# Selective-scan layers on one core: the side work of every third unit is issued ahead of the next unit's B and decay

## The chip, the cores and the metric

The kernel runs on one core of one Trainium2 chip. The metric is the device time of one execution in microseconds. It is compared with the time of the kernel before the change, run on the same chip.

The core has five engines with a queue each: TensorE (PE in the profile, PEld for its weight loads), VectorE (DVE), ScalarE (ACT), GpSimd (POOL) and SyncE (SP), which only issues DMA transfers here. An instruction waits in its engine's queue until the semaphores that it needs have been raised.

## The reference

Four layers, each adding a two-dimensional selective scan to its input `x` (8 images, 48 by 48 positions, 96 channels). Cut to what matters:

```
for each layer:
    g = group_norm(x)
    xc, z = split(g @ in_proj)                     # 192 channels each
    xc = silu(depthwise_conv3x3(xc) + conv_b)
    xs = 4 sequences of xc: by rows, by columns, and both backwards      # L = 2304
    dt, B, C = split(xs @ x_proj)                  # rank 6 or 16; 16 states; 16 states
    delta = softplus(dt @ dt_proj + bias)
    for each position, channel and state n:
        h = exp(delta * A[n]) * h + (delta * u) * B[n]
        y += h * C[n]
    y = layer_norm(sum of the 4 directions + D * u) * silu(z)
    x = x + y @ out_proj
```

The last layer writes the same recurrence with cumulative sums and an epsilon. The kernel computes it only at the two ends of each sequence, and a test at the end decides whether a full pass has to follow.

## The kernel before, in words

Images are worked in pairs. A pair's 2 x 192 channels fill three tiles of 128 partitions. For each tile there are two scan orders (rows, columns) and two directions, 12 groups in all. A group's 2,304 positions are cut into three chunks of 768. Inside a chunk a **unit** n = 0 to 15 handles one pair of states of one half of the tile: 128 partitions by 768 positions. Layers 0 to 2 ("long" layers) have 3 layers x 4 pairs x 12 groups x 3 chunks x 16 = 6,912 units. The last layer ("short") has small units of another form, which the change leaves alone.

Work of a unit in a long layer:

- `load_b` and `load` (through `fetch`, L740) have SP issue the DMAs of B and C, broadcast over the partitions. C comes for every unit, into one of nine buffers `cb`. B comes by DMA only in **pooled** units, n = 2, 5, 7, 10, 13, 15 (`pooled`), into one of three buffers `bb`.
- In pooled units POOL multiplies B by delta*u (`weigh`, L757), and ACT writes the decay exp(delta*A) into PSUM (`spread` calling `exp`, L780).
- In the other units ACT writes the decay into one of four buffers `da` (`decay`, L780). TensorE spreads B over the partitions from its bf16 parts (`spread`, L678: four matmuls into one of two PSUM buffers `b`, the same two buffers that the pooled units' decay uses). DVE multiplies B by delta*u (L810).
- `scan`: DVE runs the recurrence (L814), POOL multiplies the result by C (L823, `c*h`), and a last column is put on a list that `catch_up` has ACT copy later (L698).
- `add_up`: TensorE sums the products of a pair of units into PSUM (L870; L855 begins a sum). It runs `LAG` = 2 units behind. `collect` has ACT copy a finished sum into `y` (L887).

Beside the units run two kinds of other work, given out in small steps:

- **The softplus step** (`prepare`, a generator, `coming` in the loop) makes delta and delta*u for the next chunk but one or the next. It works on two halves of 384 columns, by steps s1 to s7 and s8 to s15: s1 and s8 the matmuls of dt (L614); s2 and s9 three ACT operations (L622 to L624); s3 and s10 three more (L626 to L628, the last two giving `w1`); s4 and s11 the matmuls of `e` and `w1` (L634, eight instructions); s5 and s12 those of `lg` and `x` (L634, eight); s6 and s13 four ACT copies of delta (L589), in s6 also the DVE product with u (L642 or L645); s14 the second half's DVE product; s7 and s15 four ACT copies of delta*u. The generator is started again at n = 15 of a chunk, where s1 is issued, and one step follows in each unit, so that s2 comes at n = 0 and s15 at n = 13.
- **The side step** (`side_step`) takes one step of the next pair's prologue (`ahead`, or `rest` at the start: input projection, the convolution's matmuls at L314, the projections and their stores) or of the last pair's epilogue (`behind`: normalization and output projection, with matmuls at L1031 to L1119, ACT operations, two DVE products at L1086 and L1108, and its loads and stores on SP). No side step is taken in the unit where `ends` holds, which is n = 2.

The order is written out by hand in `run`. One turn of its loop issues, for unit k: `collected()` (a late sum's copy), `get_ready(k + 1)` (loads for units k+5 and k+4, spread of unit k+1, weigh and decay of unit k+3), `catch_up()`, `scan` of unit k, `add_up` of unit k-2, and then, by `beside()`, the softplus step and the side step. Where a late sum has been copied (n = 3), `beside()` stands ahead of `add_up`. `keep_order` adds a dependency from each instruction of an engine to the one before it for all of the long layers, so that each engine runs them in the order in which the program issues them.

Of the kernel before, what the change touches and what calls it, by code (L numbers as in the profile page):

```python
# [103 lines left out]
def ss2d_layers_kernel(ctx: ExitStack, tc: tile.TileContext, x_in, consts, weights, out):  # L104
# [470 lines left out]
    def load_dt(c):  # L575
        r = layers[c.l].rank
        c.dts = sm1.tile([64, SCAN], F32, name="dts", tag="dts")
        for b in c.batches:
            q0 = 32 * b if c.t == 2 else 0
            nc.sync.dma_start(  # L580
                c.dts[q0 : q0 + r, : c.m],
                state[c.l, c.p]["xd"][c.ph, b, c.d * r : (c.d + 1) * r, c.c0 : c.c0 + c.m],
            )
# [101 lines left out]
    def store_some(n):  # L685
        for _ in range(min(n, len(late_stores))):
            o, z, at = late_stores.pop(0)
            nc.sync.dma_start(o[:, at], z[:, at])

    def collected():  # L690
        some = bool(late_sums)
        while late_sums:
            late_sums.pop(0)()
        return some

    def catch_up():
        while late_act:
            nc.scalar.copy(*late_act.pop(0))  # L698
# [450 lines left out]
    def drain(g):  # L1149
        for _ in g:  # L1150
            pass

    def step(g):
        next(g, None)
# [7 lines left out]
    def side_step(*sides):  # L1162

        for s in sorted(sides, key=lambda s: (not s.held, s.made / s.total)):
            got = next(s.g, s)
            s.held = got is True
            if got is not s and got is not GATED:
                s.made += 1
                return True
        return False  # L1170
# [3 lines left out]
    def mark():  # L1174
        marks.append(len(tc._region_blocks()[0].instructions))
# [12 lines left out]
    LAG = 2  # L1188
    LOADS, DECAYS = 3, 2

    def run(pairs, short):


        def units():
            for l, p in pairs:
                for gi, (t, ph, d) in enumerate(groups):
                    if l in short:
                        c = Edge(l, p, t, ph, d)
                        for i in range(NS // QUAD):
                            yield (l, p, gi * (NS // QUAD) + i), c, i  # L1200
                        continue
                    group = {}
                    for i in range(len(SCANS)):
                        c = Chunk(l, p, t, ph, d, i, group, c if d == 1 and i == 0 else None)
                        for n in range(NS):
                            yield (l, p, (gi * len(SCANS) + i) * NS + n), c, n

        def begin(l, p, first=False):
            if l not in layers:
                layers[l] = Layer(l)  # L1210
            return prologue(l, p, l in short, first)

        todo = list(units())

        def rest_of_sum(k):
            before = todo[k - 1][1] if k > 0 else None
            if isinstance(before, Chunk) and (k == len(todo) or todo[k][1] is not before):
                before.add_up(NS)

        def get_ready(k):  # L1220

            def early(ahead, what):
                for i in range(0 if k == 0 else k + ahead, min(k + ahead + 1, len(todo))):
                    getattr(todo[i][1], what)(todo[i][2])

            early(LOADS + 1, "load_b")
            early(LOADS, "load")
            if k == 0:
                todo[0][1].decay(todo[0][2])
            if k < len(todo):  # L1230
                (l, p, _), c, n = todo[k]
                if n == 0 and c.first and l not in short:
                    c.group["carry"] = capool.tile([P, NS], F32, name="carry", tag="carry")
                c.spread(n)
            early(DECAYS, "weigh")
            for i in range(k + DECAYS if k else 1, min(k + DECAYS + 1, len(todo))):
                todo[i][1].decay(todo[i][2])

        rest = begin(*pairs[0], first=True)
        while next(rest) is not READY:  # L1240
            pass
        rest = Side(rest)
        chunks = list(dict.fromkeys(c for _, c, _ in todo))
        drain(prepare(chunks[0]))
        behind = ahead = Side()
        coming = iter(())
        done = None
        mark()
        get_ready(0)
        for k, ((l, p, unit), c, n) in enumerate(todo):  # L1250
            at = pairs.index((l, p))
            following = pairs[at + 1] if at + 1 < len(pairs) else None
            if l in short and unit == 0:
                mark()
            per = NS // QUAD if l in short else NS
            all_units = len(groups) * (per if l in short else len(SCANS) * per)
            place["tiles"] = 3 * unit // all_units
            store_some(1)
            if done:
                behind, done = Side(epilogue(*done), 199), None  # L1260
            if unit == LAG and following:
                ahead = Side(begin(*following), 311)
            if k == 0:
                coming_to = 1
                coming = prepare(chunks[coming_to])
            if n == max(0, per - 1 - DECAYS):
                while coming_to < len(chunks) and not chunks[coming_to].ready:
                    next(coming)
            if n == 10 and coming_to + 1 < len(chunks):
                z = chunks[coming_to + 1]  # L1270
                if (z.l, z.p) == (l, p):
                    load_dt(z)
            busy = collected()
            get_ready(k + 1)
            catch_up()
            c.scan(n)
            if n == per - 1:
                drain(coming)
                if unit + 1 + per == all_units:
                    drain(behind.g)  # L1280
                    drain(ahead.g)
                coming_to = chunks.index(c) + 2
                coming = prepare(chunks[coming_to]) if coming_to < len(chunks) else iter(())


            def beside():
                step(coming)

                for _ in range(10 if l in short else 0 if ends else 1):
                    side_step(rest) or side_step(behind, ahead)  # L1290

            ends = l not in short and k > LAG and todo[k - LAG][2] == 0
            if busy and l not in short:
                beside()
            if k >= LAG:
                (bl, bp, _), b, bn = todo[k - LAG]
                rest_of_sum(k - LAG)
                if bl in short:
                    collected()
                b.add_up(bn)  # L1300
                if k > LAG and todo[k - LAG - 1][0][:2] != (bl, bp):
                    done = todo[k - LAG - 1][0][:2]
            if not (busy and l not in short):
                beside()
        for i in range(len(todo) - LAG, len(todo)):
            collected()
            rest_of_sum(i)
            todo[i][1].add_up(todo[i][2])
            catch_up()
        collected()  # L1310
        rest_of_sum(len(todo))
        collected()
        drain(epilogue(*pairs[-1]))

    last = NLAYER - 1
    run([(l, p) for l in range(NLAYER) for p in range(NPAIR)], (last,))

    keep_order(*marks[:2])
# [8 lines left out]
    with tc.If(nc.values_load(again, min_val=0, max_val=1) > 0):  # L1327
        run([(last, p) for p in range(NPAIR)], ())
# [95 lines left out]
```

## Time and profile before

| what | value |
|---|---|
| median of 3 runs | 20,188.83 us (20,176.15 to 20,194.05) |
| the profiled execution's own time | 20,200.44 us, its span 20,198.6 us |
| PE busy | 16,790.8 us, 83% of the span |
| PE weight loads busy | 7,792.6 us, 39% |
| DVE busy | 17,667.0 us, 87% |
| ACT busy | 16,224.6 us, 80% |
| POOL busy | 17,769.4 us, 88% |
| moved by DMA | 4,200.8 MB, 208 GB/s over the span |
| L823 on POOL, 128x768 | 1.82 us each |
| L814 on DVE, 128x768 | 1.74 to 1.81 us each |
| L810 on DVE, 128x768 | 0.95 us each |
| L780 on ACT, 128x768 | 0.93 us into `da`, 0.90 us into PSUM |

The long layers take the first 90% of the span; in the last tenth, the short layer, DVE and POOL are far less busy, so the shares of the whole span understate the long layers. In the profile an instruction stands under its engine and line with the tiles that it writes and reads, "b<-du,b" for an instruction that writes `b` from `du` and `b`. "Idle before, releaser" is the time that the engine stood still ahead of such instructions, and what ended it. In the waits view a line reads: who waited, for whom, microseconds in total, how many times, the longest.

### The profile page before, as it was taken

What the parts mean: (1) busy time and instruction counts of PE and PEld (TensorE: products, weight loads), DVE (VectorE), ACT (ScalarE), POOL (GpSimd) and SP (SyncE); (2) the same over time, 40 slices, a digit from 0 to 9 for tenths busy, and PEclk for the clock granted to TensorE, in tenths of its full rate; (3) what the DMA queues carried; (4) which work ended last, traced back from release to release, by engine and by line L of the source; (5) the groups of instructions that cost most, each with busy time, mean ns of one, the idle gap of its engine ahead of it and who ended that gap; (6) DMA issues with size and microseconds to landing.
All of it is one profiled execution on the core that took longest, in us unless ns stands there. A gap on an engine that the chain in (4) does not pass through costs nothing.

```text
span 20198.6 us, 314848 instructions
## 1 busy us (share of the span) xinstructions
PE 16790.8 (83%) x92962; PEld 7792.6 (39%) x92962; DVE 17667.0 (87%) x14161; ACT 16224.6 (80%) x30014; POOL 17769.4 (88%) x10121
## 2 busy tenths in 40 slices
PE   7888887887888888888887888888888887888886
PEld 3333333333333333333333333333333333334565
DVE  6999998998999999999999999999999999996553
ACT  6777887887887887887887887877877887887786
POOL 6999999999999999999999999999999999995442
PEclk9998998998998998998998999998999998999997
DMA  5888888888888888888888888888888888884221
GB/s 157 231 224 223 226 222 221 227 223 220 225 226 224 224 231 224 223 228 223 225 228 223 223 225 226 223 226 221 221 224 222 222 225 221 220 222 117 79 74 50
DMA packets 2021150, 4200.80 MB, mean 208 GB/s; under 512 B 375920, under 2 KB 789360, under 8 KB 2017904
## 3 DMA queue, kind: packets, MB, share of 16 engines
q1 hardware_dynamic: 2019440, 4180.55, 79.2%
q8 instruction: 762, 12.48, 0.3%
q14 instruction: 948, 7.77, 0.2%
HBM read 4026.64 MB, written 152.27 MB: 207 GB/s over the span
## 4 chain that ended last, share of the span: by engine, by line
PE 21%; ACT 17%; DVE 14%; DMA 10%; issue 9%; POOL 3%; SPq 2%; DVEq 0%; POOLq 0%; ACTq 0%
DVE da L814 7%; PE acc L870 5%; PE ps L634 4%; DMA bb<-xd 4%; DVE b L810 4%; DMA cb<-xd 4%; ACT b L780 3%; ACT dl L589 3%; PE ps L314 2%; PE b L678 2%; ACT du L589 2%; POOL cb L823 2%; DVE bb L814 2%; ACT da L780 2%; SPq L740 1%
## 5 line engine op out<-in xcount | busy, mean ns | idle before, releaser
L823 POOL TENSOR_TENSOR cb<-cb,da 128x768 f32<-128x768 f32 x4320 | 7835.9, 1819 | 749.3 <-issue 253.1
L870 PE MATMUL acc<-cb,twin 128*64 128x384 f32 x27648 | 7200.8, 539 | 721.3 <-POOL cb L823 704.5
L814 DVE TENSOR_TENSOR_SCAN da<-da,carry,b 128x768 f32<-128x768 f32 x2880 | 5223.2, 1814 | 176.0 <-DVE b L810 0.9
L757 POOL TENSOR_TENSOR bb<-bb,du 128x768 f32<-128x768 f32 x2592 | 4716.9, 1820 | 222.2 <-DMA bb<-xd 125.6
L823 POOL TENSOR_TENSOR cb<-cb,bb 128x768 f32<-128x768 f32 x2592 | 4706.8, 1816 | 100.2 <-DVE bb L814 50.7
L810 DVE TENSOR_TENSOR b<-du,b 128x768 f32<-128x768 f32 x4320 | 4085.6, 946 | 690.2 <-PE b L678 604.2
L678 PE MATMUL b<-brow,pick 96*64 96x512 bf16 (+2 forms) x18816 | 2852.5, 353 | 1886.2 <-DVE da L814 1528.4
L780 ACT ACTIVATE da<-dl,a 128x768 f32<-128x768 f32 x4320 | 4011.3, 930 | 213.5 <-POOL cb L823 183.0
L870 PEld LDWEIGHTS acc<-cb,twin 128*64 128x64 f32 x27648 | 2452.5, 149 | 2998.4 <-POOL cb L823 1333.5
L814 DVE TENSOR_TENSOR_SCAN bb<-b,carry,bb 128x768 f32<-128x768 f32 x1728 | 3109.6, 1800 | 106.0 <-ACT b L780 35.6
L780 ACT ACTIVATE b<-dl,a 128x768 f32<-128x768 f32 x2592 | 2335.3, 901 | 623.2 <-DVE da L814 598.4
L678 PEld LDWEIGHTS <-pick 96*64 96x64 bf16 x18816 | 1077.9, 115 | 4164.4 <-DVE da L814 2717.6
L814 DVE TENSOR_TENSOR_SCAN da<-da,b 128x768 f32<-128x768 f32 x1440 | 2525.3, 1754 | 87.4 <-DVE b L810 1.4
L314 PE MATMUL ps<-pad,diag 128*64 128x480 f32 (+1 forms) x8640 | 2339.7, 567 | 34.6 <-ACT du L589 24.4
L589 ACT COPY dl<-ps 64x384 f32<-64x384 f32 x3456 | 1632.6, 472 | 697.9 <-PE ps L634 659.6
L589 ACT COPY du<-ps 64x384 f32<-64x384 f32 x3456 | 1633.5, 473 | 200.7 <-DVE ps L645 109.8
L634 PE MATMUL ps<-du,cst 128*64 128x384 f32 (+1 forms) x7296 | 1704.5, 506 | 76.5 <-ACT du L628 65.6
L814 DVE TENSOR_TENSOR_SCAN bb<-b,bb 128x768 f32<-128x768 f32 x864 | 1502.1, 1739 | 145.5 <-ACT b L780 92.2
L634 PE MATMUL ps<-dl,cst 128*64 128x384 f32 (+1 forms) x7296 | 1485.2, 483 | 0.0
L614 PE MATMUL ps<-dts,w 6*128 6x384 f32 (+5 forms) x2432 | 961.4, 605 | 205.0 <-DMA dts<-xd 105.4
L622 ACT ACTIVATE du<-ps,w 128x384 f32<-128x384 f32 (+1 forms) x912 | 519.9, 570 | 714.6 <-PE ps L614 701.0
L314 PEld LDWEIGHTS ps<-pad,diag 128*64 128x64 f32 x8640 | 751.8, 139 | 885.0 <-issue 729.6
(144 smaller groups left out, 19166.4 us busy)
## 6 DMA issues: line engine op xcount, KB each, us to landing
cb<-xd SPq DMA_DIRECT2D x13952, 192.0 KB
bb<-xd SPq DMA_DIRECT2D x5184, 192.0 KB
brow<-xb SPq DMA_DIRECT2D x864, 72.0 KB
ey<-yd SPq DMA_DIRECT2D x256, 216.0 KB
cb<-xd SPq DMA_DIRECT2D x128, 384.0 KB
yd<-y SPq DMA_DIRECT2D x216, 192.0 KB
ex<-xs SPq DMA_DIRECT2D x256, 108.0 KB
xb<-parts SPq DMA_DIRECT2D x96, 216.0 KB
```

Of the source, the lines that this page charges most:

```text
L314: nc.tensor.matmul(ps[half, :m], ly.diag[:, int(t == 2), j, half], pad[:, r0 + dy : r0 + dy + nr, dx : dx + W], start=(j == 0), stop=(j == 8),
L589: nc.scalar.copy(z[64 * h : 64 * h + 64, g, at], v[64 * g : 64 * g + 64])
L614: nc.tensor.matmul(o[:, :m], ly.dtw[q0 : q0 + r, k, chans], dts[q0 : q0 + r, at], start=True, stop=True,)
L622: nc.scalar.activation(e, v, AF.Abs, bias=bias)
L634: nc.tensor.matmul(v[half], ident[:, half], z1, start=(i == 0), stop=(i == 3))
L678: nc.tensor.matmul(o[64 * h : 64 * h + 64], pick[:, b, n : n + 1].to_broadcast([2 * NR, 64]), rows, start=True, stop=True,)
L757: nc.gpsimd.tensor_mul(b, b, self.du[n % 2])
L780: nc.scalar.activation(da, self.dl[n % 2], AF.Exp, scale=layers[self.l].a2[:, int(self.t == 2), n % 2, k, i : i + 1],)
L810: nc.vector.tensor_mul(b, self.du[n % 2], b)
L814: nc.vector.tensor_tensor_scan(way(h), way(da), way(b), start, ALU.mult, ALU.add)
L823: nc.gpsimd.tensor_mul(c, c, h)
L870: nc.tensor.matmul(self.acc[64 * g : 64 * g + 64, a, : self.m // 2], twin, c[:, a, :], start=False, stop=(pair + 2 == NS and not self.turns),)
```

## The change

In units of a long layer whose B comes from DRAM (the pooled ones), the softplus step and the side step are issued ahead of `get_ready(k + 1)` instead of behind `add_up`. `ends` is computed earlier for that, and the side step gets a name, `aside`. In the unit n = 15 the softplus generator is started again after the scan as before, and its first step is issued right there, ahead of `add_up`. The other units keep their order, and no instruction is added or taken away.

```diff
+            def aside():
+                side_step(rest) or side_step(behind, ahead)
+
             busy = collected()
+            ends = l not in short and k > LAG and todo[k - LAG][2] == 0
+
+            ahead_of_b = l not in short and c.pooled(n)
+            if ahead_of_b:
+                if n < per - 1:
+                    step(coming)
+                if not ends:
+                    aside()
             get_ready(k + 1)
             catch_up()
             c.scan(n)
@@
                 coming_to = chunks.index(c) + 2
                 coming = prepare(chunks[coming_to]) if coming_to < len(chunks) else iter(())
 
+                if ahead_of_b:
+                    step(coming)
 
             def beside():
                 step(coming)
 
                 for _ in range(10 if l in short else 0 if ends else 1):
-                    side_step(rest) or side_step(behind, ahead)
-
-            ends = l not in short and k > LAG and todo[k - LAG][2] == 0
+                    aside()
+
             if busy and l not in short:
                 beside()
             if k >= LAG:
@@
-            if not (busy and l not in short):
+            if not (busy and l not in short) and not ahead_of_b:
                 beside()
```

## The prediction

> **What bounds the kernel now.** I read the windows view first, for one stretch of the three long layers: the busy time of each engine, the share of the TensorE clock granted, the DMA share and GB/s.
>
> ```profile
> core 0: us, PE busy (x) PEld busy (x) DVE busy (x) ACT busy (x) POOL busy (x), PEclk, DMA share, GB/s
> 1000.00:18000.00 17000.00, 14187.28 (x76949) 6261.55 (x76946) 15712.38 (x11823) 13854.57 (x25612) 15985.16 (x9064) 0.91 0.86 224
> ```
>
> POOL works 94% of this stretch, DVE 92%, TensorE 83%, ACT 81%. No engine is full; the two fullest are tied to one another by every unit, since POOL's product `c*h` needs DVE's scan. So the waits of DVE come next, from the waits view of the whole run:
>
> ```profile
> PE b L678 <- DVE da L814: 1528.4, 1125, 6.1
> PEld acc L870 <- POOL cb L823: 1333.5, 1033, 4.6
> DVE b L810 <- PE b L678: 604.2, 623, 10.5
> POOL bb L757 <- DMA bb<-xd: 125.6, 107, 4.0
> ```
>
> The third line is the place of the change. DVE's multiply waits 604 us for the spread matmuls (L678), by far its largest wait. The first line is the other side: the spread waits 1,528 us for DVE's scan to free one of the two PSUM buffers of B. TensorE is sometimes early at the spread and sometimes late, and it matters in which unit of the 16.
>
> So I numbered the 6,912 scans (L814) in order of time, took the number modulo 16 as the unit n, and averaged over the 432 chunks. A chunk lasts 41.8 us (18,062 us for 432). DVE's wait before its multiply is 0.61 us at n=1, 0.42 at n=11, 0.15 at n=6, 0.14 at n=12, 0.11 at n=0, 0.08 at n=3 and under 0.05 elsewhere. At n=1, 6, 9 and 14 POOL has caught up: its `c*h` starts within a median of 0.22 us after the scan. A delay of DVE therefore reaches POOL, and the end, within a chunk. I take DVE as the pacing engine.
>
> **What the Trainium skill says.** "Perfetto Trace Analysis", section "Per-instruction lifecycle: what the profiler-reported window actually captures", says that ACT, DVE and GpSimd are strict FIFO, and that TensorE's queue only pulls weight loads ahead of running matmuls. The trace agrees: L678, L870 and L634 run in program order in every chunk I looked at. An instruction placed ahead of the spread therefore delays it if TensorE is not idle there. The same page, "Optimization Strategy", tells to find the gaps of the most contended engine and what releases them; that is the count above. The same page calls TensorE's ends an estimate, so I use starts of the next instruction where I can.
>
> **The change part by part.** In long units with n = 2, 5, 7, 10, 13, 15 one softplus step and one side step move from behind `add_up` to ahead of `get_ready`. Their matmuls now precede spread(n+1); nothing is removed. The unit after a pooled one is never pooled, so the moved work always meets a spread. That spread may start when scan(n-1) ends and is needed when scan(n) ends, 1.8 us later.
>
> *n=10.* The softplus steps fall on fixed units: s1 at n=15, s2 at 0, up to s15 at 13. At n=10 it is s12: eight L634 matmuls. This is a chunk in the TensorE view, then the same time on DVE (start, duration, engine, line):
>
> ```profile
> 7324.60 0.54 PE L870 MATMUL acc<-cb,twin 128*64 128x384 f32 x1 [1.30 <-POOL cb L823]
> ...
> 7325.05 1.38 PE L634 MATMUL ps<-du,cst 128*64 128x384 f32 x6
> ...
> 7326.83 0.38 PE L678 MATMUL b<-brow,pick 96*64 96x512 bf16 x1
> ...
> 7328.12 1.38 PE L634 MATMUL ps<-dl,cst 128*64 128x384 f32 x6
> 7329.09 0.57 PE L314 MATMUL ps<-pad,diag 128*64 128x480 f32 x1
> ```
>
> ```profile
> 7325.96 1.79 DVE L814 TENSOR_TENSOR_SCAN bb<-b,carry,bb 128x768 f32<-128x768 f32 x1
> 7327.92 0.96 DVE L810 TENSOR_TENSOR b<-du,b 128x768 f32<-128x768 f32 x1 [0.17 <-PE b L678]
> ```
>
> add_up(7) waits for POOL, s11 and side(9) follow, and spread(11) starts at 7326.83, already so late that the multiply at 7327.92 waits. After the change s12 (1.46 us for eight) and side(10) stand in between. Over all chunks the moved TensorE work at n=10 is 2.13 us busy, and TensorE has no idle time to hide it (0.04 us before spread(11)). For each chunk I add the moved time to the moment TensorE was free, start the spread at the later of that and scan(9)'s end, add the spread's own time, and compare with the end of scan(10). The same sum without the move gives 0.45 us where 0.42 is seen. With it: 2.44 us. That is +2.0 us a chunk, **+860 us**.
>
> *n=2.* The step is s4, the matmuls of e and w1; no side step moves here (`ends`). w1 comes from ACT's s3:
>
> ```profile
> 6643.56 0.62 ACT L628 ACTIVATE du<-du,ones 128x384 f32<-128x384 f32 x1
> ```
>
> ```profile
> 6643.88 0.51 PE L678 MATMUL b<-brow,pick 96*64 96x512 bf16 x4
> 6644.23 0.81 PE L870 MATMUL acc<-cb,twin 128*64 128x384 f32 x4
> 6644.88 1.46 PE L634 MATMUL ps<-du,cst 128*64 128x384 f32 x8
> ```
>
> Now spread(3) and add_up(0) run while w1 is being finished. Afterwards s4 is first, so spread(3), and DVE behind it, wait for ACT: this is an added wait. w1 ends 0.88 us after scan(1) on average (tenth to ninetieth percentile -0.12 to 1.63); its four matmuls and the spread follow. The same sum gives 1.14 us of wait instead of 0.09: **+455 us**.
>
> *n=5, 7, 13.* Their softplus steps are ACT work, so only the side step's matmuls move, 0.50 to 0.60 us. At 5 the slack is small: +111 us; at 7: +56; at 13 TensorE idles 1.1 us before the spread: +1. Together **+168 us**.
>
> *n=15.* Here the move helps. TensorE idles 2.05 us before spread(0), so side(15), 0.82 us, fits for nothing; s1 stays behind the scan and only passes add_up(13). Spread(1) is no longer behind side(15): the 0.61 us wait at n=1 loses the smaller of itself and the moved time, 0.32 us: **-136 us**. The wait at n=0 goes by the same sum: -46. At n=12 the late multiply of n=11 gives the spread more time and the 0.14 us goes: -58. Together **-240 us**. What is late next in the chunk is s4 at n=2.
>
> *DVE.* Side steps hold the epilogue's products L1086 and L1108, which now come before scan(n) instead of behind it, with ACT's half issued just one unit earlier. 112 of them fall on moved units; the end of their ACT input against scan(n-1) gives 187 us where 25 was paid: **+162 us**. The bound is zero to this.
>
> *ACT and POOL.* ACT's part passes a decay that is three units early and a carry copy that waits for the scan: nothing, covered by the 0.48 us a unit that ACT idles (18.5% of 2.61). Bound: -100 us (the wait of scans for the pooled exp, 128 us in all) to +100. POOL's few residual subtractions: nothing.
>
> *SP.* The side steps' DMA issues (ex, ey, xs, xd, xb, some 310 on moved units) now pass two issues of C and, at times, two of B, and their wait holds these one unit sooner. C is issued four units, about 10 us, ahead. I take nothing; bound: zero to +150 us (the present waits of POOL's weigh for DMA are 126).
>
> *Sum.* 860+455+168+162-240 = +1,405 us. A slower DVE gives the others time: its waits for ACT copies, pooled exps and DMA, some 290 us, may lose half (-145). POOL, having less backlog, frees add_up(7) sooner: -100, my estimate. Rounded: **+1,120 us**. The profiled execution took 20,200.4 us (span 20,198.6), 12 us over the median of 20,188.8, so I forecast about **21,310 us**, 5.6% slower.
>
> **Rivals.** *A, faster.* The moved work fills TensorE's idle time ahead of spreads. For it: 1,528 us of waits for the scan, and 0.53 us at n=8, 1.1 at 14, 2.05 at 0. Against: 0.04 us at n=11 and 0.23 at n=3, where the large steps go. It decides if TensorE reaches s12 more than 2 us sooner than now; then the waits at n=1, 12, 0 and 11 go (265+58+46+180, by 432 chunks), -0.55 ms: 19,640 us; with the relief of n=15 alone, 19,950. *B, POOL's backlog pays.* POOL lags the scan by 0.93 us at n=11 and 1.27 at n=3; if this hid as much delay each time, n=3 costs nothing and n=11 1.07 us: 20,650 us. Against it: POOL has caught up again by n=14. *C, SP as well.* The loads come late too: +300 us on my sum, 21,600. *D, nothing moves,* because the order is not kept: `keep_order` ties each engine to program order, so hardly.
>
> **How the numbers follow.** Forecast, with C as its upper end, 0.70; B 0.15; A 0.12; none 0.03. 0.2% is about what a measurement of this kernel can tell from no change. Slower 0.85, same 0.03, faster 0.12. The range goes from 20,450, which leaves A, D and a little of B out, to 21,750.
>
> **What would show it.** Right: the DVE wait for PE L678 grows from 604 us to some 1,800, with 2 us and more at n=11 and about 1 at n=3; s12's L634 starts before spread(11); n=1 waits about 0.3; POOL's busy share falls to some 89%. Wrong: DVE's wait does not grow, or it does and the span doesn't (then POOL set the pace), or POOL's wait for `bb` rises by several hundred us (then it was SP).

## The result and the profile after

The changed kernel takes a median of 21,176.86 us (21,150.55 to 21,190.02) against 20,191.44 us (median of six runs) of the kernel before on the same chip: 985 us more, a ratio of 1.0486 with a 95% interval of 1.0473 to 1.0500. The profiled execution has a span of 21,148.7 us, 950 more than the one before.

The windows view of the long layers comes first, with the columns of the one before: the stretch, its length, the busy time of PE, PEld, DVE, ACT and POOL, the clock, the DMA share, GB/s.

```profile
1000.00:18800.00 17800.00, 14321.33 (x76520) 6289.88 (x76518) 15659.64 (x11756) 13738.20 (x25479) 15917.70 (x9010) 0.89 0.80 213
```

No engine became the bound: POOL falls from 94% to 89% of the stretch, DVE from 92% to 88%, TensorE from 83% to 80%, DMA from 0.86 to 0.80. All of them wait more. The waits view of the whole run says who for:

```profile
PE b L678 <- DVE da L814: 1531.3, 927, 7.1
...
DVE b L810 <- PE b L678: 1205.5, 876, 10.7
...
DVE eyc L1086 <- ACT ps L1084: 298.4, 93, 16.1
...
DVE b L810 <- PE acc L870: 258.7, 133, 6.5
...
DVE eyc L1108 <- ACT ps L270: 162.2, 79, 7.4
...
POOL bb L757 <- DMA bb<-xd: 73.2, 66, 4.5
```

DVE's multiply now waits 1,205.5 + 258.7 = 1,464 us; both lines are the multiply behind its spread (in the second an L870 matmul ended close by and got the name), and before they held 604.2 and 76.0. The first line, TensorE's wait for the scan, has hardly changed in total (1,528.4 before): on balance the moved work did not use up that idle time. POOL's wait for B's transfer fell from 125.6 to 73.2 us, so the DMA queue is not the cause.

The pattern of n=10 and 11, in the TensorE view and then on DVE, for the chunk that the prediction showed:

```profile
7698.09 0.54 PE L870 MATMUL acc<-cb,twin 128*64 128x384 f32 x1 [1.22 <-POOL cb L823]
...
7700.64 1.38 PE L634 MATMUL ps<-dl,cst 128*64 128x384 f32 x6
7701.60 0.56 PE L314 MATMUL ps<-pad,diag 128*64 128x480 f32 x1
...
7702.41 0.38 PE L678 MATMUL b<-brow,pick 96*64 96x512 bf16 x1
```

```profile
7699.64 1.79 DVE L814 TENSOR_TENSOR_SCAN bb<-b,carry,bb 128x768 f32<-128x768 f32 x1
7703.50 0.96 DVE L810 TENSOR_TENSOR b<-du,b 128x768 f32<-128x768 f32 x1 [2.08 <-PE b L678]
```

s12's L634 and the convolution's L314 stand between add_up(7) and spread(11). The spread starts 2.8 us after the start of scan(10), where it started 0.9 us after it, and DVE's wait grows from 0.17 to 2.08 us.

And n=2 in one chunk, in the views of ACT, TensorE and DVE:

```profile
7191.12 0.61 ACT L628 ACTIVATE du<-du,ones 128x384 f32<-128x384 f32 x1
```

```profile
7191.79 0.87 PE L634 MATMUL ps<-du,cst 128*64 128x384 f32 x4 [0.91 <-ACT du L628]
7192.48 0.50 PE L678 MATMUL b<-brow,pick 96*64 96x512 bf16 x4
```

```profile
7193.02 0.96 DVE L810 TENSOR_TENSOR b<-du,b 128x768 f32<-128x768 f32 x1 [0.47 <-PE b L678]
```

TensorE stands 0.91 us for ACT's w1, the spread is behind it, and DVE waits for the spread.

The table counts DVE's wait before the multiply by unit, in us a chunk, with the numbering of the scans that the prediction used. In a chunk 0.1 us is 43 us of the run. Pooled units have no such multiply, and n=4 stays at 0.05 us or less.

| kernel | n=0 | 1 | 3 | 6 | 8 | 9 | 11 | 12 | 14 |
|---|---|---|---|---|---|---|---|---|---|
| before | 0.11 | 0.61 | 0.08 | 0.15 | 0.04 | 0.01 | 0.42 | 0.14 | 0.00 |
| after | 0.07 | 0.39 | 0.72 | 0.15 | 0.14 | 0.00 | 1.82 | 0.00 | 0.10 |
| e1, without 10 | 0.13 | 0.43 | 0.82 | 0.15 | 0.16 | 0.00 | 0.48 | 0.14 | 0.04 |
| e2, without 2 and 10 | 0.14 | 0.42 | 0.07 | 0.36 | 0.12 | 0.01 | 0.54 | 0.14 | 0.04 |
| e3, softplus step only | 0.09 | 0.67 | 0.55 | 0.06 | 0.02 | 0.01 | 1.12 | 0.00 | 0.00 |
| e4, side step only | 0.14 | 0.30 | 0.11 | 0.36 | 0.18 | 0.01 | 0.81 | 0.04 | 0.03 |
| e5, w1 last | 0.08 | 0.39 | 0.34 | 0.13 | 0.14 | 0.00 | 1.76 | 0.00 | 0.10 |
| e6, one unit later | 0.14 | 0.08 | 0.47 | 0.00 | 0.00 | 0.39 | 0.05 | 0.11 | 0.00 |
| e7, sides moved | 0.19 | 0.29 | 0.06 | 0.18 | 0.05 | 0.02 | 0.27 | 0.08 | 0.00 |
| e8, both | 0.54 | 0.00 | 0.50 | 0.00 | 0.00 | 0.69 | 0.06 | 0.16 | 0.00 |
| e9, product apart | 0.16 | 0.73 | 0.08 | 0.29 | 0.01 | 0.26 | 0.07 | 0.16 | 0.00 |
| e10, and a side moved | 0.54 | 0.46 | 0.13 | 0.35 | 0.01 | 0.25 | 0.05 | 0.14 | 0.00 |
| e11, only 15 | 0.14 | 0.39 | 0.08 | 0.18 | 0.03 | 0.02 | 0.46 | 0.13 | 0.00 |
| e12, only 10 | 0.04 | 0.52 | 0.06 | 0.15 | 0.03 | 0.02 | 1.86 | 0.00 | 0.00 |

One thing neither the prediction nor an experiment dealt with: the share of its full clock that TensorE is granted falls too, from 0.91 to 0.89 in the windows views. In the traces' record of the clock this share is either 1 or one half. Up to the end of the last long layer's scans it is one half for 3,284 of 18,297 us before, and for 4,118 of 19,247 us after. An L870 of 128x384 is shown with 0.49 us on average where it starts at full clock and with 0.83 us at half clock. This is a stretch of the kernel before at half clock, in the windows view (the clock is 0.50), then the spread of a unit n=1 in it on TensorE, after an L870 group from just ahead of the stretch, and the multiply on DVE:

```profile
6549.80:6556.50 6.70, 6.70 (x30) 4.05 (x28) 5.46 (x5) 5.91 (x12) 5.71 (x4) 0.50 0.57 163
```

```profile
6548.65 0.81 PE L870 MATMUL acc<-cb,twin 128*64 128x384 f32 x4
...
6552.86 0.85 PE L678 MATMUL b<-brow,pick 96*64 96x512 bf16 x4
6553.51 1.49 PE L870 MATMUL acc<-cb,twin 128*64 128x384 f32 x4
```

```profile
6553.76 0.96 DVE L810 TENSOR_TENSOR b<-du,b 128x768 f32<-128x768 f32 x1 [1.10 <-PE b L678]
```

Is the slower clock the loss? All waits before the multiply, sorted by the clock at the start of their spread, come to 259 us at full and 431 us at half clock before, and to 1,024 and 455 us after. So nearly all that was added stands at full clock; at n=11 the wait there grows from 0.27 to 1.76 us. But the clock does mark where the kernel before waited: at n=1, 1.01 us in the 257 chunks where spread(1) starts at half clock, and 0.02 us in the other 175. No run here sets the clock, so how much of those older waits it causes stays open.

### The profile page after: what moved, and what is told of

It reads as the page before. It is cut to its first block, busy times and chain, and to the rows that moved or that the text cites. A ratio compares the mean times of both kernels' runs of the same rounds, so it can differ in the third digit from the quotient of the medians.

```text
span 21148.7 us, 315415 instructions
## 1 busy us (share of the span) xinstructions
PE 17007.3 (80%) x92962; PEld 7846.3 (37%) x92962; DVE 17708.0 (84%) x14161; ACT 16178.5 (76%) x30014; POOL 17797.5 (84%) x10121
## 4 chain that ended last, share of the span: by engine, by line
PE 21%; ACT 20%; DVE 16%; issue 8%; DMA 7%; POOL 3%; SPq 2%; DVEq 0%; POOLq 0%; ACTq 0%
DVE da L814 7%; PE ps L634 5%; DVE b L810 5%; PE acc L870 5%; ACT b L780 4%; ACT da L780 4%; DMA cb<-xd 3%; ACT du L589 3%; PE ps L314 2%; ACT dl L589 2%; PE b L678 2%; POOL cb L823 2%; DVE bb L814 2%; DMA bb<-xd 2%; SPq L740 1%
## 5 line engine op out<-in xcount | busy, mean ns | idle before, releaser
L870 PE MATMUL acc<-cb,twin 128*64 128x384 f32 x27648 | 7039.6, 556 | 693.6 <-POOL cb L823 691.7
L810 DVE TENSOR_TENSOR b<-du,b 128x768 f32<-128x768 f32 x4320 | 4090.0, 947 | 1478.7 <-PE b L678 1205.5
L757 POOL TENSOR_TENSOR bb<-bb,du 128x768 f32<-128x768 f32 x2592 | 4707.7, 1816 | 137.8 <-DMA bb<-xd 73.2
L678 PE MATMUL b<-brow,pick 96*64 96x512 bf16 (+2 forms) x18816 | 2807.8, 357 | 1939.2 <-DVE da L814 1531.3
L870 PEld LDWEIGHTS acc<-cb,twin 128*64 128x64 f32 x27648 | 2385.0, 153 | 3266.8 <-issue 1524.3
L678 PEld LDWEIGHTS <-pick 96*64 96x64 bf16 x18816 | 1162.9, 118 | 4070.7 <-DVE da L814 2310.7
L589 ACT COPY du<-ps 64x384 f32<-64x384 f32 x3456 | 1634.4, 473 | 1102.3 <-DVE ps L645 564.2
L314 PE MATMUL ps<-pad,diag 128*64 128x480 f32 (+1 forms) x8640 | 2219.4, 566 | 84.6 <-ACT u L322 32.1
L634 PE MATMUL ps<-du,cst 128*64 128x384 f32 (+1 forms) x7296 | 1915.1, 530 | 273.3 <-ACT du L628 254.6
L589 ACT COPY dl<-ps 64x384 f32<-64x384 f32 x3456 | 1632.1, 472 | 387.3 <-PE ps L634 351.2
L634 PE MATMUL ps<-dl,cst 128*64 128x384 f32 (+1 forms) x7296 | 1534.5, 493 | 0.0
L314 PEld LDWEIGHTS ps<-pad,diag 128*64 128x64 f32 x8640 | 755.6, 140 | 963.5 <-issue 768.7
L634 PEld LDWEIGHTS ps<-du,cst 128*64 128x64 f32 x7296 | 680.5, 149 | 1076.8 <-ACT du L628 507.1
```

Of the source, the lines that this page charges most:

```text
L314: nc.tensor.matmul(ps[half, :m], ly.diag[:, int(t == 2), j, half], pad[:, r0 + dy : r0 + dy + nr, dx : dx + W], start=(j == 0), stop=(j == 8),
L589: nc.scalar.copy(z[64 * h : 64 * h + 64, g, at], v[64 * g : 64 * g + 64])
L634: nc.tensor.matmul(v[half], ident[:, half], z1, start=(i == 0), stop=(i == 3))
L678: nc.tensor.matmul(o[64 * h : 64 * h + 64], pick[:, b, n : n + 1].to_broadcast([2 * NR, 64]), rows, start=True, stop=True,)
L757: nc.gpsimd.tensor_mul(b, b, self.du[n % 2])
L810: nc.vector.tensor_mul(b, self.du[n % 2], b)
```

## The experiments

The theory (M): the loss is made where a step's matmuls, or their wait for ACT, stand in front of a spread that has no idle time ahead of it, so above all at n=10 and n=2. The rivals: each moved unit costs alike, by a queue such as SP's (E, S); or the pace is POOL's and DVE's waits are not what the time is made of (P). The kernel before was timed beside each group of runs on the same chip: 20,212.19 us for e1 to e4, 20,194.38 for e5 to e8, 20,191.70 for e9 to e12. Losses and gains below are taken from these.

**e1 and e2: units 10, then 2 and 10, put back.**

```diff
-            ahead_of_b = l not in short and c.pooled(n)
+            ahead_of_b = l not in short and c.pooled(n) and n != 10            # e1
+            ahead_of_b = l not in short and c.pooled(n) and n not in (2, 10)   # e2
```

> The change, except that unit n=10 keeps the old order. Theory M (matmuls in front of the spread): nearly all of the loss of n=11 comes back. Its wait goes from 1.82 us a chunk to about 0.42 (432 chunks: -605 us), n=12 gets its 0.14 us back (+59), n=14 loses its 0.10 (-45): 20,590 us. Rival E (each of the six moved units costs about alike, through queues such as SP's): a sixth of 985 us comes back, 21,010 us.

> The change, except that units n=2 and n=10 keep the old order. Theory M: the wait at n=3 falls from 0.72 us to 0.08 as well (-276 us), 20,310 us; what is left over the kernel before is the DVE products (about 130 us) and n=8, less the gain at n=1. Rival E: a third of the loss comes back, 20,850 us.

Measured: e1 20,716.23 us, a ratio of 1.0251 (1.0234 to 1.0268) to the kernel before; e2 20,460.42 us, 1.0126 (1.0109 to 1.0143). Their losses are 504 and 248 us, where the change loses 985. So the unit n=10 gives back 481 us and n=2 another 256 us; two of six units hold 737 of 985 us, and E, which wanted 165 each, falls. Both gave back less than M expected (590 and 276). At e2 the table shows one reason: with the wait of n=3 gone, n=6 rises from 0.15 to 0.36. A wait gives TensorE time, which the next late spread uses. For the 248 us that are left, the trace shows DVE idle 156 us longer than before ahead of its products L1086 and L1108, and 127 us longer ahead of the multiplies (n=6, 8 and 11 wait longer, n=1 less).

**e12 and e11: unit 10 alone, unit 15 alone.**

```diff
+            ahead_of_b = l not in short and c.pooled(n) and n == 10            # e12
+            ahead_of_b = l not in short and c.pooled(n) and n == 15            # e11
```

> The change in unit n=10 alone. Theory M: n=11 waits 1.9 us instead of 0.42, n=12 loses its 0.14: +580 us, 20,770 us, about what is lost when the other five units move too and n=10 gets back its place (480 us). Rival E (units cost alike): a sixth of 985, 20,355 us.

> The change in unit n=15 alone, the unit where the prediction saw a gain. Theory M: the wait at n=1 falls by about 0.2 us (-85 us), but the epilogue's products that now stand in front of scan(15) wait 0.2 us a chunk for ACT, as they do in the changed kernel (+80 to +100 us): 20,190 us, no difference. Rival G (the gain of n=1 stands alone): 20,100 us.

e12 measured 20,611.15 us, 1.0207 (1.0190 to 1.0224): 419 us more. From its waits view, with 604.2 and 76.0 us on the same two lines before:

```profile
DVE b L810 <- PE b L678: 896.2, 590, 9.3
...
DVE b L810 <- PE acc L870: 275.5, 128, 6.2
```

The wait of n=11 grew by 1.44 us a chunk, 622 us, but the waits at n=12, 1 and 0 shrank by 59, 41 and 30 us. DVE's smaller waits shrank by another 46 us; the last 27 us are not placed. Unit 10 holds 419 us alone and 481 us among the others: the places add up to within some 60 us.

e11 measured 20,153.55 us, 0.9983 (0.9976 to 0.9990). Unit 15 is a small gain of 38 us, between the two expectations (20,190 and 20,100). Its n=1 wait fell by 0.22 us a chunk (96 us), and in the same trace L1086 and L1108 in front of scan(15) wait 0.19 us a chunk (83 us).

**e3 and e4: one kind of step alone.**

```diff
                 if n < per - 1:
                     step(coming)
-                if not ends:            # e3: aside() stays behind add_up in these units
-                    aside()
...
```

```diff
-                if n < per - 1:         # e4: step(coming) stays behind add_up in these units
-                    step(coming)
                 if not ends:
                     aside()
...
```

> Only the softplus step goes ahead in the six units, the side step stays behind the sum. So no side DMA and no epilogue product of DVE moves. Theory M: s12 (1.46 us) and s4 still stand in front of spread(11) and spread(3): wait at n=11 about 1.2 us, at n=3 about 0.7, none at n=12, the gain of n=1 mostly gone: 20,750 us. Rival S (the side steps' DMA issues on SP, or their DVE products, are the loss): about 20,190 us.

> Only the side step goes ahead in the six units, the softplus step stays behind the sum. Theory M: wait at n=11 about 0.8 us (+160 us), nothing at n=3, some 0.1 us more each at n=6, 8, 14 (+90), DVE products +134, n=1 -97, n=12 -40: 20,440 us. Rival S (side DMA issues on SP, or the products): nearly the whole loss, 21,180 us.

Measured: e3 20,708.83 us, 1.0249 (1.0232 to 1.0266); e4 20,632.32 us, 1.0213 (1.0196 to 1.0230). With no side DMA and no product moved, e3 still loses 497 us, and neither kernel has the whole loss, so S falls. The waits at n=11 (1.12 and 0.81 us) are as M had them (1.2 and 0.8). e4 lost 420 us where M said 250: n=6 rose by 0.21 us and not by 0.1, since nothing at n=3 made TensorE time, and the scan of n=7 itself waits 0.18 us a chunk longer than before (78 us), mostly for ACT's pooled exp, which M did not have.

**e5: is n=3's wait ACT's or the matmuls' own time?**

```diff
-            for i, z1 in enumerate((e, w1, lg, x)):
+            for i, z1 in enumerate((e, x, lg, w1)):
```

> The change, and in the softplus steps the order of the four summed terms is e, x, lg, w1 instead of e, w1, lg, x, so that s4 at n=2 no longer needs ACT's last result. Theory A (the wait at n=3 is in part TensorE standing behind ACT's w1): that wait falls from 0.72 us to about 0.35, the part that is s4's own 1.46 us; some 0.1 us comes up at n=6: 21,060 us. Theory T (it is s4's matmul time alone): no change, 21,180 us.

Measured: 20,936.42 us, 1.0368 (1.0350 to 1.0385), a loss of 742 us, 243 less than the change. The wait at n=3 is 0.34 us, as theory A said (0.35), and T falls. What TensorE waited for ahead of L634, weight loads and matmuls counted together, in the changed kernel and then in this one:

```profile
  ACT du L628: 761.8, 635
```

```profile
  ACT du L628: 19.3, 52
```

That the rest of n=3's wait is the matmuls' own time fits this, and is not shown apart. The gain is larger than expected (120 us): the wait of n=3 makes 166 of it, n=11 another 27; the last 50 us are not placed.

**e6, e7, e8: the same theory used the other way, on the kernel before.**

```diff
             def beside():
-                step(coming)
+                if l in short or n < per - 1:                                          # e6, e8
+                    step(coming)
...
+                sides = 2 if n in (13, 14) else 0 if n in (9, 15) else 1               # e7
+                sides = 2 if n in (13, 14) else 0 if n in (4, 15) else 1               # e8
-                for _ in range(10 if l in short else 0 if ends else 1):
+                for _ in range(10 if l in short else 0 if ends else sides):
```

> The kernel before, with the softplus steps one unit later (s1 at n=0 to s15 at n=14), all of them behind the sum. Theory M (a spread is late where matmuls of a softplus step stand in front of it): s11 no longer precedes spread(11), so the wait of n=11 (0.42 us) goes; s1 no longer precedes spread(1), n=1 falls from 0.61 to about 0.3; s5 now precedes spread(6) more closely, n=6 rises from 0.15 to about 0.4: 20,020 us. Rival P (POOL's 94% set the pace, DVE's waits are not what the time is made of): 20,190 us.

> The kernel before, with side steps given out unevenly: none in units 9 and 15, two in units 13 and 14, so that they run where TensorE idles ahead of spread(0). Theory M: wait at n=1 0.61 to about 0.3, at n=11 0.42 to about 0.1: 19,960 us. Rival P: 20,190 us.

> The kernel before, softplus steps one unit later as in the run above, and no side step in units 4 and 15, two in 13 and 14. Theory M: waits at n=1 about 0.1, at n=11 none, at n=6 0.15 as before: 19,820 us. Rival P: 20,190 us.

e6 measured 20,675.28 us, 1.0231 (1.0214 to 1.0248); e8 21,160.61 us, 1.0472 (1.0454 to 1.0489). Both expectations missed by far, and not to P's side. The waits at n=1 and 11 did go. But s6, ACT's copies and DVE's product in one step, came into n=5. In the kernel before, the copies start with the scan of their unit (0.10 us after its start on average) and end 0.23 us after it does. In e6 ACT first stands 1.72 us a chunk for s5's matmuls, the copies start 2.00 us after the start of scan(5), and DVE, whose next instruction is the product, waits for all 1.9 us of them. From the waits view of e6 (659.6, 62.6 and 131.1 us for these before):

```profile
ACT dl L589 <- PE ps L634: 888.7, 607, 4.6
...
DVE ps L645 <- ACT dl L589: 554.3, 217, 5.5
...
DVE ps L642 <- ACT dl L589: 475.8, 214, 75.6
```

DVE stands some 2.2 us a chunk there. M, which looks at spreads alone, did not have this wait; what e6 supports is the wider statement that a wait of DVE costs time, whoever causes it. The rises at n=3 and n=9 stand almost wholly at half clock (1.47 and 0.60 us there, 0.07 and 0.03 us at full clock). e8 loses another 485 us: n=0 rises by 0.40 and n=9 by 0.30 us a chunk over e6, and the products L1086 and L1108 in front of scan(15) wait 0.32 us, some 440 us in all.

e7 measured 20,132.69 us, 0.9969 (0.9958 to 0.9979), a gain of 62 us where 230 was expected. n=1 fell as said (0.29); n=11 only to 0.27, perhaps since s11 and a wait for POOL's product are still ahead of it; L1086 and L1108 in front of scan(15) take back 0.20 us a chunk.

**e9 and e10: s6 split instead.**

```diff
             to_twins(dl, at, v)
             if z + m == c.m:
                 if l == NLAYER - 1:
                     c.sum_up()
                 c.ready = True
-                yield
+            yield                                                                      # e9, e10
             times_u(v)
...
+                sides = 2 if n == 14 else 0 if n == 15 else 1                          # e10
-                for _ in range(10 if l in short else 0 if ends else 1):
+                for _ in range(10 if l in short else 0 if ends else sides):
```

> The kernel before, with the first half's DVE product with u in a softplus step of its own, one unit behind ACT's copies, as the second half has it; all later softplus steps come one unit later. Theory M: s11's matmuls no longer stand in front of spread(11), so the wait of 0.42 us there goes, and so does DVE's wait of 0.24 us for ACT's copies at n=5: 432 x 0.66 = 285 us, 19,910 us. Rival P (POOL's 94% leave less than that): 20,050 us or more.

> As the run above, and the side step of unit 15 is given out in unit 14, behind its sum, so that it runs in the idle time ahead of spread(0). Theory M: the wait at n=1 also falls from 0.61 to about 0.3 us, less some 0.1 us for DVE products at n=15: 19,820 us. Rival P: no better than the run above.

e9 measured 20,033.35 us, 0.9924 (0.9907 to 0.9940), the fastest of all here: 0.8% under the kernel before. The wait at n=11 went (0.07), and DVE's wait for ACT's copies fell from 62.6 us to this, ahead of L645:

```profile
  ACT dl L589: 5.9, 10
```

Of the 285 us expected 158 came: n=1, 6 and 9 rose by 0.11, 0.14 and 0.24 us (212 us in all). For n=9 this fits s8's matmuls, which now stand ahead of spread(9): the wait is 0.86 us in the 109 chunks where that spread starts at half clock and 0.05 us in the others. For n=1 and 6 no reason is shown. In its windows view POOL works 94.8% of the stretch:

```profile
1000.00:18000.00 17000.00, 14440.85 (x77616) 6273.69 (x77614) 15801.92 (x11928) 13948.59 (x25844) 16114.94 (x9152) 0.92 0.85 226
```

Rival P's bound of 20,050 lies inside the interval (20,004 to 20,071 us), so e9 does not decide on P; that three waits came up is enough for what stayed away, but a POOL so near to full is not ruled out as a part of it. e10 measured 20,200.26 us, 1.0006 (0.9997 to 1.0015), and M missed: n=1 fell to 0.46, but with two side steps in unit 14 spread(0) is late, n=0 rose from 0.16 to 0.54, and the products in front of scan(15) wait 0.25 us a chunk. The clock shows where: spread(0) starts at half clock in 127 of the 432 chunks (68 in e9), and the multiply waits 1.64 us there, 0.09 us in the others.

Of the five uses of the theory on the kernel before, e7 and e9 brought 62 of 230 and 158 of 285 us, e10 brought nothing, and e6 and e8 were slower. So M accounts for the loss of this change; it is not enough to say what another order will gain.

## Why the prediction was right, point by point

It forecast 21,310 us; 21,177 was measured, by the mechanism named. The terms, with the DVE waits of the trace in place of the estimates (each times 432):

- **n=10:** forecast +860 us, a wait of 2.44 us at n=11. Measured 1.82 us, +604. The step was mis-sized: 2.13 us of counted TensorE time were added to the modelled end of the matmul before the spread. But spread(11) starts 0.25 us ahead of that modelled end before the change (0.27 after), and the moved work put it off by 1.89 us only. Its starts in the old trace, all put 1.89 us later and nothing else changed, give a wait of 1.88 us.
- **n=2:** forecast +455, measured +276 (0.72 us, not 1.14). The added wait for w1 is there, as e5 shows, but the same modelled ends were used; spread(3) starts 0.20 us ahead of them. How the rest of the difference comes about stays open.
- **n=5, 7, 13:** forecast +168, measured +89, and elsewhere than said: nothing at n=6, where +111 was forecast, 45 each at n=8 and 14. Each unit was worked out alone; e2 and e4 show n=6 at 0.36 us where n=3 does not wait.
- **n=15, 0, 12:** forecast -240, measured -97, -16 and -59, that is -172.
- **DVE products:** forecast +162. The waits view gives +54 and +77, that is +131.
- **ACT, POOL, SP:** taken at nothing. SP right: POOL's wait for B fell. The moved ACT copies of delta*u do wait for DVE (the row "ACT du L589 <- DVE ps L645" goes from 110 to 564 us), and no loss from it shows; ACT has idle time. Not foreseen: DVE's scans at n=7 and 15 wait about 60 us for POOL, where 4 were paid; the reason stays open.
- **What the others give back:** forecast -245, half of DVE's other waits and an earlier add_up(7). This did not come: the waits for ACT's copies stayed (131.1 to 137.6 on L642), and all waits ahead of scans together fell by 18 us, the 60 us for POOL included.
- **The sum itself:** 1,405 less 145 and 100 is 1,160; the prediction rounded it to 1,120 and gave no reason for the 40 us.

DVE's own account is whole: from its first scan to its last the profiled execution is 957 us longer than before, and DVE is 915 us longer idle, 788 of it ahead of the multiply, 136 ahead of L1086 and L1108, 11 ahead of L642 and L645, and 18 less ahead of the scans. DVE's work being nearly the same, its idle time must grow by about what the kernel loses; so this shows where the time went, and that the moved steps are the cause rests on the runs that put them back. The forecast of +1,120 was near in part by luck: n=10 and n=2 together were 435 us too large, and 285 us that did not come, or had no reason, were taken off.

Of the rivals, B (POOL's backlog pays, 20,650) falls by the measured time and by POOL's idle time: its wait ahead of `c*h` at n=11 grew from 0.13 to 1.03 us a chunk. A (faster) falls by the measured time; C by the wait for B. The signs named in the prediction came, most of them smaller: 1.8 us at n=11 (2 and more was said), 0.7 at n=3 (about 1), 0.39 at n=1 (0.3), POOL at 89%. DVE's wait for PE L678 was to grow from 604 to some 1,800 us; that row is 1,205.5, and 1,464 with the row under the name of L870. The gain at n=1 was put down to the place of side(15) alone; that this wait stands at half clock was not seen.

On the pages of the Trainium skill: that ACT, DVE and GpSimd are strict FIFO, and that TensorE's queue can pull weight loads ahead of matmuls under way ("Perfetto Trace Analysis", section "Per-instruction lifecycle: what the profiler-reported window actually captures"), carries the explanation. The runs agree: in e5 an exchange of two operands alone, after which TensorE no longer stands for w1, took back 243 us. The order that the prediction read from the trace holds for groups of matmuls; single matmuls of neighbouring groups start among each other, as the last section shows. The same section calls TensorE's ends an estimate; here the next start lies 0.2 to 0.3 us ahead of them.

## What to carry to other kernels

Before work is moved ahead of an instruction in an in-order queue, look up, place by place in the loop's period, how long the engine idles just there; a total does not tell, as 1.5 ms of idle TensorE time did not hide 2.1 us of work at n=10. Count what a moved step waits for as well as its own time, and check who stands behind it. Add such places up in order, not each alone: a wait in one place makes slack for the next, and taking it away shows the next one. Sort a place's waits by the granted clock as well: here the one at n=1 in the kernel before stands almost wholly at half clock.

## What was not expected of the hardware

Eight L634 matmuls, each shown with a median of 0.486 us, take 1.46 us together where nothing runs among them (the group at 6644.88 in the prediction's view). There they start in pairs, some 3 ns apart within a pair, 0.32 us from pair to pair, so each pair starts 0.16 us ahead of the modelled end of the last. Matmuls of one group also start among those of the next, as L678, L314 and L870 do at 7702.41 and after. The cost of a moved group is therefore the shift of the next group's start and neither the sum of the durations nor the modelled ends: 1.89 us for spread(11) (2.91 after the end of scan(9), 1.02 before), with 2.13 us counted as busy.

The half clock is not spread evenly over the loop's period: in the kernel before spread(1) starts at half clock in 257 of 432 chunks, spread(6) in none and spread(12) in one. The reason stays open.
